# A short GpSimd memset behind each of 64 indirect transfers

## The chip, the cores and the metric

The kernel runs on one core of a Trainium2 chip. The metric is the device time of one execution in microseconds. Lower is better. The core has five engines with their own instruction queues: PE (TensorE, matmuls and transposes), DVE (VectorE), ACT (ScalarE), POOL (GpSimd) and SP (SyncE, which here only issues DMAs). Each queue runs in its written order, and semaphores order the queues against each other.

## The reference

A sequence model of four layers works on `x` of 4 x 1024 tokens x 128 features in float32. Each layer adds a mixing part and then a feed-forward part, with a layernorm behind each. Layer 1's feed-forward part and its neighbours are what matters here:

```python
x = _layernorm(x + _L1_attn_ref(...))     # a linear recurrence over the tokens
x = _layernorm(x + _L1_ffn_ref(...))      # 16 experts, 4 per token, and a shared expert
x = _layernorm(x + _L2_attn_ref(...))     # causal attention, 16 heads of 8
x = _layernorm(x + _L2_ffn_ref(...))      # 8 experts, 2 per token
```

```python
# _L1_ffn_ref, in short
topk_idx, tw = _route(x, router_w, bias)  # 4 of 16 experts from 2 of 4 groups, weights
h = einsum('td,edf->etf', x, gate_w); u = einsum('td,edf->etf', x, up_w)
y = einsum('etf,efd->etd', silu(h) * u, down_w)
routed = einsum('etd,te->td', y, combine) # combine: tw at the chosen experts
return routed + shared_expert(x)
```

The other layers are a gated scan and a quantized linear layer (layer 0), and a short Toeplitz mix with 32 experts (layer 3).

## The kernel before, in words

The tokens lie in SBUF as 32 tiles of 128 tokens. The experts are not computed for all tokens. For each layer with experts and each part of the tokens, the kernel writes a list of rows to DRAM, sorted by expert, and the experts read it back in groups of four tiles. Layer 1 has two parts: `a`, the first half of every sequence, and `r`, the second half. Their lists are called `l1ra` and `l1rr` (layer 1, rows, part). Layers 2 and 3 have three lists each.

- `l1_route` computes the router on DVE, and `positions` (line 1261) turns it into row numbers `posl1r` (line 1302).
- `spread` (line 1373) writes the list: for each of 16 tiles and each of 4 choices, one indirect DMA from `x` to the rows named by `posl1r`. That is 64 transfers of 128 rows. They are issued by `indirect` (line 1325, the DMA itself at line 1327) from the Pool queue[...].
- `gathered` (line 1388) reads a group of the list back as `xg`, by a DMA of the SP queue at line 1392. It waits for every transfer of the list, and for its buffer.
- `small_experts` (line 1781) transposes `xg` on PE (line 169) and runs the experts.

The order of work is written out by hand as generators. `mix` runs a main generator and lets a side generator step in by estimated times; whatever the side adds is ordered behind the latest instruction of the main one on the same engine. The estimate per transfer is `step`. Around the change, the main generator is layer 2's attention on the first half of the sequences, and the side is layer 1's routing and spreading of part `r`:

```python
self.run(self.mix(self.l2_attn(0), self.chain(self.l1_route(r), self.spaced(self.spread("l1", r, K1), 1, 2, 1.45))))
```

`spaced(..., 1, 2, 1.45)` sets `self.spacing`: every transfer waits for the landing of the one two before it (`before`, line 1345), and the planner counts 1.45 us for each. Part `a` is spread without it. `self.moved` holds the names of the latest transfers; each new one is ordered behind the last two of them in Pool's queue, without a semaphore. After this line come the experts of layer 1 on part `r`, with layer 2's routing and its list `l2ra` at their side.

Of the kernel before, what the change touches and what calls it, by code (L numbers as in the profile page):

```python
# [20 lines left out]
P = 128  # L21
# [35 lines left out]
class Part:  # L57
# [3 lines left out]
    def __init__(self, name, q0, nq, rows=None, lg0=None):  # L61
        self.name, self.q0, self.nq, self.lg0 = name, q0, nq, lg0
        if rows is None:
            self.order = list(range(q0 * QT, (q0 + nq) * QT))
        else:
            self.order = [tile_of(b, 2 * q + k) for b in rows for q in range(q0, q0 + nq) for k in range(2)]
        self.t0, self.nt = q0 * QT, len(self.order)
# [7 lines left out]
class Kernel:  # L75
    def __init__(self, ctx, tc, ins, out, cols, consts, rows):
        self.tc, self.nc, self.ins, self.out = tc, tc.nc, ins, out
        self.count = itertools.count()
        nc = self.nc
        self.const = self.pool(ctx, "const")  # L80
        self.small = self.pool(ctx, "small", 3)
        self.routes = self.pool(ctx, "routes")
        self.side = self.pool(ctx, "side", 2, space=PSUM)
        dram = self.pool(ctx, "dram", space=DRAM)

        self.cols_t = self.load(self.const, ins["cols"])
        self.cst_t = self.load(self.const, ins["consts"])
        self.x = self.tile(self.const, [P, NT, D], "x")
        self.xT = self.tile(self.const, [P, NT * P], "xT")
        nrow = ins["rows"].shape[1]  # L90
        self.rows_t = self.tile(self.const, [P, nrow], "rows")
        nc.gpsimd.dma_start(out=self.rows_t, in_=ins["rows"].to_broadcast([P, nrow]))
        self.col = {k: self.cols_t[:, a:b] for k, (a, b) in cols.items()}
        self.cst = {k: self.cst_t[:, a:b] for k, (a, b) in consts.items()}
        self.row = {k: self.rows_t[:, a:b] for k, (a, b) in rows.items()}
        self.ident = self.cst["ident"]
        self.eps = self.tile(self.const, [P, 1], "eps")
        nc.vector.memset(self.eps, LN_EPS)
        self.halfpi = self.tile(self.const, [P, 1], "halfpi")
        nc.vector.memset(self.halfpi, math.pi / 2)  # L100
        self.ones = self.tile(self.const, [P, E3], "ones")
        nc.vector.memset(self.ones, 1.0)
        self.rnd = self.tile(self.const, [P, 1], "rnd")
        nc.vector.memset(self.rnd, RND)
        self.drop = self.tile(self.const, [P, 1], "drop")
        nc.vector.memset(self.drop, -RND)
        self.zero = self.tile(self.const, [P, D], "zero")
        nc.gpsimd.memset(self.zero, 0.0)
        self.flag = self.tile(self.const, [1, 1], "flag", I32)
        self.hm = self.tile(self.const, [P, 4], "hmg")  # L110

        self.first, self.rest = Part("a", 0, 2), (Part("b", 2, 1), Part("c", 3, 1))
        self.parts = (self.first, *self.rest)
        self.by_rows = (
            Part("a", 0, 2, range(B), 0), Part("m", 2, 2, (0, 1), NT // 2), Part("n", 2, 2, (2, 3), 3 * NT // 4)
        )

        self.rows_done = 0

        self.listed = set()  # L120

        self.traced, self.latest = nc.cur_bb.bb.instructions, {}
        self.now = self.moved_by = 0.0
        self.moved = []
        self.landing = []
        self.spacing = None

        self.lists, self.route = {}, {}
        self.both = (self.first, Part("r", 2, 2))
        for lay, ne, k in (("l1", E1, K1), ("l2", E2, K2), ("l3", E3, K3)):  # L130
            for pt in {"l1": self.both, "l2": self.by_rows, "l3": self.parts}[lay]:
                tl = -(-((pt.nt * P * k + (P - 1) * ne) // P) // 4) * 4
                self.lists[lay, pt.name] = (
                    self.tile(dram, [tl * P, D], f"{lay}r{pt.name}"), self.tile(dram, [tl * P, D], f"{lay}y{pt.name}"), tl
                )
        self.wall2 = self.tile(dram, [P, E2 * 3 * F2], "wall2")
        self.xsave = self.tile(dram, [P, NT, D], "xsave")

        self.ksave = self.tile(dram, [P, B, BLK], "ksave")
        self.vsave = self.tile(dram, [P, B, 4, (NH + 1) * VW], "vsave")  # L140
# [1232 lines left out]
    def spread(self, lay, part, k):  # L1373

        pos, _, _, done, _ = self.route[lay + part.name]
        rows = self.lists[lay, part.name][0]
        for t in range(part.nt):
            for i in range(k):
                ins = self.indirect(
                    apart=done,  # L1380
                    out=rows, out_offset=bass.IndirectOffsetOnAxis(ap=pos[:, t, i : i + 1], axis=0),
                    in_=self.x[:, part.order[t], :], in_offset=None,
                )
                done.append(ins)
            yield (self.step * k,)
        self.listed.add(lay + part.name)

# [835 lines left out]
```

## Time and profile before

| what | value |
| --- | --- |
| median of 3 runs | 1930.79 us (1930.78 to 1932.56) |
| the profiled execution | 1937.33 us, of which the span is 1935.5 us |
| mean granted PE clock | 0.896 of full speed |
| Pool busy | 690.3 us, 36% of the span |
| transfers to `l1rr` | 64, 1022 ns of Pool each on the mean, from 629.0 to 723.7 us |

The span goes from the first to the last instruction of the profiled execution; about 1.8 us of its time lie around it. A row of the profile names the line, the engine, the operation and the tiles (output, arrow, inputs), then how many there were, how long they were busy in all, and the mean of one in ns. Idle time stands behind it with what ended it: a landing of a DMA, an instruction of another engine, or "issue" where the profile shows no wait. For a DMA, the row of the issuing engine only covers the issue; the landing comes later.

### The profile page before, as it was taken

What the parts mean: (1) busy time and instruction counts of PE and PEld (TensorE: products, weight loads), DVE (VectorE), ACT (ScalarE), POOL (GpSimd) and SP (SyncE); (2) the same over time, 40 slices, a digit from 0 to 9 for tenths busy, and PEclk for the clock granted to TensorE, in tenths of its full rate; (3) what the DMA queues carried; (4) which work ended last, traced back from release to release, by engine and by line L of the source; (5) the groups of instructions that cost most, each with busy time, mean ns of one, the idle gap of its engine ahead of it and who ended that gap; (6) DMA issues with size and microseconds to landing.
All of it is one profiled execution on the core that took longest, in us unless ns stands there. A gap on an engine that the chain in (4) does not pass through costs nothing. (4 is left out here: it accounts for less than half of the span.)

```text
span 1935.5 us, 27095 instructions
## 1 busy us (share of the span) xinstructions
PE 1541.5 (80%) x9025; PEld 920.8 (48%) x9025; DVE 1199.2 (62%) x3491; ACT 900.6 (47%) x1349; POOL 690.3 (36%) x670
## 2 busy tenths in 40 slices
PE   7885677597847887989977878798798998999850
PEld 3332433385423345856632232333355757768650
DVE  8998698465766664635564565546442446866383
ACT  5876265243324554423336756564532236644330
POOL 2000148604630660265443000030536430567775
PEclk9897688798978998999988988898988999989985
DMA  9990002244430113632241000000452213425452
GB/s 297 288 288 10 1 17 86 87 126 133 159 129 18 60 63 129 183 96 73 78 137 32 1 1 1 2 23 1 159 213 83 66 28 93 141 68 167 122 147 61
DMA packets 215530, 187.10 MB, mean 97 GB/s; under 512 B 16528, under 2 KB 194064, under 8 KB 214864
## 3 DMA queue, kind: packets, MB, share of 16 engines
q1 hardware_dynamic: 194672, 142.29, 23.6%
q0 software_dynamic: 20704, 42.86, 7.3%
q8 instruction: 84, 1.38, 0.3%
q14 instruction: 70, 0.57, 0.1%
HBM read 88.49 MB, written 96.60 MB: 96 GB/s over the span
## 5 line engine op out<-in xcount | busy, mean ns | idle before, releaser
L1081 ACT ACTIVATE pr<-sc 128x1024 f32<-128x1024 f32 x288 | 279.4, 1021 | 175.2 <-PE sc L161 174.8
L161 PE MATMUL sc<-qm,kT 32*128 32x512 f32 (+3 forms) x1536 | 197.7, 559 | 16.7 <-ACT pr L1081 16.7
L161 PE MATMUL s<-pr,va 128*32 128x512 f32 (+3 forms) x1536 | 167.5, 532 | 19.0 <-DVE x L1019 10.2
L161 PE MATMUL gu<-ld,xgT 128*128 x640 | 165.1, 400 | 10.2 <-DVE hg L1812 5.9
L1087 DVE TENSOR_TENSOR pr<-pr,ld 128x512 f32<-128x512 f32 (+1 forms) x160 | 91.7, 581 | 105.6 <-ACT pr L1081 105.4
L161 PE MATMUL gu<-wall,xgT 128*128 x304 | 148.2, 612 | 2.0 <-ACT xgT L171 2.0
L161 PEld LDWEIGHTS sc<-qm,kT 32*128 32x128 f32 x1536 | 83.7, 194 | 112.4 <-issue 61.1
L161 PEld LDWEIGHTS gu<-ld,xgT 128*128 128x128 f32 x640 | 119.5, 198 | 34.7 <-DVE hg L1812 6.1
L1812 DVE TENSOR_TENSOR hg<-sg,gu 128x256 f32<-128x256 f32 x160 | 66.0, 417 | 92.0 <-ACT sg L1811 91.6
L173 DVE COPY hT<-tp 128x512 f32<-128x512 f32 x118 | 80.9, 686 | 66.2 <-PE tp L169 66.2
L1567 ACT ACTIVATE sg<-gu 128x512 f32<-128x512 f32 x76 | 45.4, 597 | 144.7 <-PE gu L161 143.6
L1811 ACT ACTIVATE sg<-gu 128x256 f32<-128x256 f32 x160 | 61.3, 385 | 107.7 <-PE gu L161 79.8
L171 ACT COPY xgT<-tp 128x512 f32<-128x512 f32 x99 | 58.0, 586 | 99.9 <-PE tp L169 99.8
L1327 POOL DMA_INDIRECT l1ra<-x,posl1a x64 | 79.8, 1246 | 61.3 <-DVE peq L1321 42.0
L1327 POOL DMA_INDIRECT l1rr<-x,posl1r x64 | 65.4, 1022 | 100.9 <-DVE posl1r L1302 70.8
L169 PEld LDWEIGHTS tp<-ld,hg 128*128 128x128 f32 x624 | 77.4, 141 | 49.0 <-issue 32.5
L1569 DVE TENSOR_TENSOR hg<-sg,gu 128x512 f32<-128x512 f32 x76 | 51.8, 682 | 78.9 <-ACT sg L1567 78.8
L1327 POOL DMA_INDIRECT l2rm<-x,posl2m x16 | 15.7, 983 | 236.8 <-DVE peq L1320 230.1
L169 PE MATMUL tp<-ld,hg 128*128 128x128 f32 x624 | 96.4, 275 | 3.7 <-DVE hg L1812 2.0
L1327 POOL DMA_INDIRECT l3ra<-x,posl3a x64 | 63.7, 996 | 93.3 <-DVE usedl3a L1315 51.0
L161 PEld LDWEIGHTS s<-pr,va 128*32 128x32 f32 x1536 | 37.1, 113 | 122.6 <-issue 78.4
L161 PE MATMUL yp<-ld,hT 128*128 x640 | 86.1, 276 | 2.3 <-DVE mv L197 1.5
(447 smaller groups left out, 3439.1 us busy)
## 6 DMA issues: line engine op xcount, KB each, us to landing
wall<-wall SPq DMA_DIRECT2D x16, 768.0 KB, 7.8
l3ra<-zero SPq DMA_DIRECT2D x1, 6144.0 KB, 25.5
ld<-in_l_w SPq DMA_DIRECT2D x2, 3072.0 KB, 10.6
wall<-we SPq DMA_DIRECT2D x24, 256.0 KB, 2.1
ld<-in_l_w SPq DMA_DIRECT2D x1, 6144.0 KB, 20.6
l1ra<-zero SPq DMA_DIRECT2D x1, 5120.0 KB, 19.6
l1rr<-zero SPq DMA_DIRECT2D x1, 5120.0 KB, 23.1
xg<-l3ra SPq DMA_DIRECT2D x20, 256.0 KB, 2.9
```

Of the source, the lines that this page charges most:

```text
L161: return self.nc.tensor.matmul(out, lhsT, rhs, start=start, stop=stop)
L169: nc.tensor.transpose(pt[:, k * P : (k + 1) * P], s, self.ident)
L171: nc.scalar.copy(dst, pt[:, : n * P])
L173: nc.vector.tensor_copy(dst, pt[:, : n * P])
L1081: nc.scalar.activation(pr, sc[h], AF.Exp)
L1087: nc.vector.tensor_tensor(d, d, cst["tril"].unsqueeze(1).unsqueeze(1).to_broadcast([P, 2, n, P]), ALU.mult)
L1327: ins = self.nc.gpsimd.indirect_dma_start(**kw)
L1567: nc.scalar.activation(sg, gu[:, 0, :], AF.Silu)
L1569: nc.vector.tensor_tensor(h, sg, gu[:, 1, :], ALU.mult)
L1811: nc.scalar.activation(sg, pg[:, :, 0, :], AF.Silu)
L1812: nc.vector.tensor_tensor(h[:, 2 * c : 2 * c + 2, :], sg, pg[:, :, 1, :], ALU.mult)
```

## The change

A tile `idle` of 384 bytes per partition is added. Behind each transfer of the list `l1r` (layer 1, part `r`), and only where the spacing is set, Pool clears this tile with a memset. The memset is ordered behind its transfer, and, by its entry in `self.moved`, ahead of the next transfer, both without a semaphore. Nothing reads the tile.

```diff
@@ __init__
         self.eps = self.tile(self.const, [P, 1], "eps")
+        self.idle = self.tile(self.const, [P, 384], "idle", mybir.dt.uint8)
         nc.vector.memset(self.eps, LN_EPS)
@@ spread
                 done.append(ins)
+                if lay + part.name in ("l1r",) and self.spacing:
+                    stay = self.nc.gpsimd.memset(self.idle, 0)
+                    self.tc.add_manual_dep(
+                        stay.ins, ins.ins.name,
+                        mybir.DependencyInfo(mybir.DependencyClass.NoSync, mybir.DependencyReason.DATA),
+                        reason="queued behind",
+                    )
+                    self.moved.append(stay.ins.name)
             yield (self.step * k,)
```

## The prediction

> **What bounds the kernel now.** I read the page first, then the Pool timeline around the list that is touched, then the waits of the DMA queue that reads the list, then PE's timeline at the point where the list is first used.
>
> ```profile
> span 1935.5 us, 27095 instructions
> PE 1541.5 (80%) x9025; PEld 920.8 (48%) x9025; DVE 1199.2 (62%) x3491; ACT 900.6 (47%) x1349; POOL 690.3 (36%) x670
> ...
> L1327 POOL DMA_INDIRECT l1rr<-x,posl1r x64 | 65.4, 1022 | 100.9 <-DVE posl1r L1302 70.8 <-DMA l1rr<-x,posl1r 23.8 <-issue 6.4
> ```
>
> PE is the busiest engine; Pool is busy for a third of the span. The 64 transfers of layer 1's second list, l1rr, cost Pool 65.4 us of work, and 23.8 us of waiting are put down to landings. Pool's own timeline in that stage (start, duration, idle before):
>
> ```profile
> 635.58 0.95 POOL L1327 DMA_INDIRECT l1rr<-x,posl1r  x1 [0.30 <-DMA l1rr<-x,posl1r]
> 637.28 0.95 POOL L1327 DMA_INDIRECT l1rr<-x,posl1r  x1 [0.75 <-DMA l1rr<-x,posl1r]
> 640.50 0.95 POOL L1327 DMA_INDIRECT l1rr<-x,posl1r  x1 [2.26 <-DMA l1rr<-x,posl1r]
> 641.75 1.02 POOL L1327 DMA_INDIRECT l1rr<-x,posl1r  x1 [0.30 <-issue]
> ...
> 723.65 0.96 POOL L1327 DMA_INDIRECT l1rr<-x,posl1r  x1 [0.30 <-DMA l1rr<-x,posl1r]
> 805.14 0.95 POOL L1327 DMA_INDIRECT l2ra<-x,posl2a  x1 [80.52 <-DVE posl2a L1302]
> ```
>
> The usual step is 1.26 us: 0.96 of work and a gap of 0.30 that is there whoever is named as its releaser. Only what lies above 0.30 is a true wait for a landing: eleven gaps, 11.0 us above their 0.30 in all (0.45, 1.96, 0.52, 0.73, 2.07, 0.44, 1.56, 0.31, 1.52, 0.87, 0.59). So the list runs from 629.0 to 723.65 (first and last start), 94.6 us. After it Pool has nothing to do until 805.14, and what it does then waits for DVE: no later work of Pool is queued close behind the list.
>
> Who waits for the list? The SP queue, which loads it back for the experts (xg, line 1392), and behind that PE's transposes of xg (waits as total us, times, longest):
>
> ```profile
> SPq L1392 <- DMA l1rr<-x,posl1r: 20.5, 4, 13.4
> SPq L1392 <- PE s L169: 19.5, 1, 19.5
> ...
> 745.48 2.79 SPq L1392 DMA_DIRECT2D xg<-l1rr  x3
> ...
> 754.60 1.88 PE L161 MATMUL s<-ld,t 128*128 128x8 f32 x8 [0.68 <-ACT t L171]
> 756.34 1.95 PE L169 MATMUL tp<-ld,xg 128*128 128x128 f32 x8
> ...
> 724.70:745.50 20.80, 18.22 (x196) 9.94 (x192) 12.15 (x45) 12.23 (x16) 0.00 (x0) 1.00 0.01 4
> 745.50:756.10 10.60, 3.80 (x19) 3.19 (x20) 5.50 (x28) 1.15 (x2) 0.00 (x0) 0.75 0.68 225
> ```
>
> SP first waits for the landings and then 19.5 us more for a PE transpose that frees the buffer. The list's last landing took 2.9 us from its issue (the view of l1rr from 715 to 760), so it was down at 726.6; the loads went out at 745.48 because of the buffer. The first three xg loads landed 2.9 us after issue (view of xg, 740 to 750), the first at 748.4, but PE used it at 756.1 (its weight load), without a wait, since its queue still held the tail of the attention. The stage's end is set by PE and DVE in the attention (PE busy 18.22 of 20.80 us, then the norm on DVE), not by the list. The last landing may therefore move from 726.6 to 745.5 + (756.1 - 748.4) = 753.1 before PE loses anything: **26.5 us of cover**.
>
> **The change, part by part.** It adds 64 Pool memsets of 128x384 bytes, one after each l1rr transfer, in Pool's program order. The instruction orders of PE, DVE, ACT and SP are the same apart from names, with the same waits; on Pool the memsets alternate with the transfers, and one l1rr transfer loses a wait on Pool's own counter (another wait pair, on PE and ACT, goes from a later l2ym gather; the trace shows no wait there for either). A tile of 384 bytes per partition is added. The planned step of 1.45 us per transfer is unchanged, so nothing else is moved. Queued behind each memset is only the next transfer; behind the last one, l2ra, 57 us later than anything here.
>
> What is one memset worth? The nearest rows:
>
> ```profile
> L344 POOL MEMSET keep<- 128x1024 f32 x1 | 1.0, 955 | 0.0
> L108 POOL MEMSET zero<- 128x128 f32 x1 | 0.2, 232 | 0.0
> L2213 POOL MEMSET const-uint8-127<- 128x1 uint8 x1 | 0.1, 103 | 0.0
> ...
> 7.43 0.95 POOL L344 MEMSET keep<- 128x1024 f32 x1
> 8.44 0.10 POOL L345 MEMSET keep<- 128x4 f32 x1
> ```
>
> Slope (955 - 232) / 896 = 0.807 ns per f32 element; 384 elements are 232 + 256 x 0.807 = 439 ns. That takes a byte as dear as a word. If the bytes went as 96 words it would be about 0.20 us: the low end. The high end is 0.50 + 0.30 = 0.80, where the transfer's 0.30 gap is paid once more on the way into and out of the memset. No row shows a memset between two indirect transfers.
>
> First rule weighed. The row's duration gives 0.44 per memset. The Trainium skill, "Perfetto Trace Analysis", section "GPSIMD Engine Instruction", says that a GpSimd row's span is not to be trusted and that one should take start-to-start distances. In this trace that is 8.44 - 7.43 = 1.01 against a duration of 0.955, so 0.06 more: 0.50. The sum by each: the list has 63 steps; a transfer waits for the landing of the one two before it, so two memsets lie in every such wait and take away up to twice their length from each of the eleven waits. With 0.44: 63 x 0.44 = 27.7, less 7.4 taken away, 20.3 us longer, 6.2 of the cover left. With 0.50: 31.5 less 7.9, 23.6 us longer, 2.9 left. I take 0.50, the dearer: last transfer at 747.3, landed at 750.2, first xg at 753.1, PE needs it at 756.1. **Cost on the path: nothing**; the cover is the buffer's release at 745.48 and PE's queue up to 756.1. At 0.20 the list grows by 8.3 us, at 0.80 by 50.4 - 10.2 = 40.2, which is 13.7 past the cover. The cover is used up at 0.55 per memset (34.6 - 8.3 = 26.3), and 0.2% (3.9 us, about what a measurement of this kernel can tell from no change) is reached at 0.62. That is a thin margin: 0.05 us per memset is 3 us.
>
> Second rule weighed, one that speaks against the change. DVE's rows in the stage: L964 tensor_scalar takes 482 ns at the median and 622 at most, L213 346 and 546, with Pool busy for 65 of 95 us; over the 16 of them (means 498 and 390 ns) that is 8 x 0.016 + 8 x 0.044 = 0.5 us above the medians. The Trainium skill, "SBUF — State Buffer", section "Who interferes with whom", says that DVE in a two-port mode and GpSimd lock each other out for a whole instruction. By the rule all 20 such DVE instructions between 629 and 748 could wait a whole memset, 20 x 0.5 = 10 us, some of it before PE transposes; by the row, 32 us more of Pool work adds 0.5 x 32 / 65 = 0.25 us. I take the row. The other way round, Pool's transfers were lengthened by 4 us over their 0.96; the memsets may be too by a share (2 us), which would eat most of the 2.9 left.
>
> Sum: the profiled execution took 1937.33 us (span 1935.5 and 1.8 around it); the runs' median is 1930.79. Only the difference is carried over: 0 for the memsets, about 1 us for brushes with DVE and the thin margin: 1932.
>
> **The rivals.**
>
> *The memset costs more than 0.62 us each, and the list becomes the bound.* One mechanism: each hand-over between transfer and memset pays the 0.30 gap again. The place is SP's wait for the last landing at line 1392 and then PE's first transpose of xg at 756.1. With 0.80 the last landing is at 766.8 and PE starts 13.7 us late; the stage behind it has PE busy 68.5 of 73.9 us and would not make it good: 1930.8 + 13.7 = 1944.5. For it: every transfer here shows that 0.30 even with nothing to wait for. Against: around the direct transfers at the kernel's start the next memset begins with no gap. It decides from 0.55, and counts from 0.62.
>
> *Faster, by the granted clock.* In 745.5 to 756.1 the clock is 0.75, in the 59 us before the list 0.82, over the whole run 0.896. Shifted work can meet the half-speed phases elsewhere; the same program took 6.5 us more in the profiled execution than in the median run, so moves of this size occur. 5 us less: 1926. Against: nothing in the change saves work, and waits of Pool that vanish here were not on the path.
>
> *The change does not do what it says.* The memsets could be so short (0.20) that only the landing waits are filled: 1930.8. It gives the forecast's side.
>
> **How the numbers follow.** Hidden or nearly so (memset below 0.62): 0.46. List past its cover by more than 3.9 us: 0.39, since the margin is thin and three small costs point one way; most of it between 1935 and 1945. Faster by clock: 0.15. The likeliest is 1932, its own range 1927 to 1934.6. The range that holds 8 in 10 takes in the rival at 0.80 nearly whole, and most of the clock's: 1927 to 1944.
>
> **What would show it.** Right: memset rows of about 0.44 us, l1rr steps near 1.76 us, last transfer near 747, landing waits above 0.30 down to about 3 us, xg loads a few us after 745.5, PE's first tp<-ld,xg without a wait on DMA xg at about 756. Wrong: steps above 1.9 us, PE waiting for DMA xg at that transpose, or DVE's tensor_scalar rows clearly above 0.48 us in the stage. A difference with none of these would have to be in the clock row.

## The result, and the profile after

| kernel | median | runs |
| --- | --- | --- |
| before | 1933.76 us (1927.75 to 1941.34) | 14 |
| with the memsets | 1939.64 us (1935.14 to 1947.70) | 14 |

The ratio is 1.0039, 95% interval 1.0024 to 1.0053: slower by about 7 us on the means, and the whole interval lies above 1. The profiled execution took 1947.7 us, the longest of the 14, so its own excess (10 us over the profiled one of before) is larger than the typical one.

One fact has to be known before the experiments are read. Chips differ: the same kernel before takes about 1930 us on the chips of this table and on chip 4, and about 2250 us on chips 3, 10 and 14. Every ratio below is against the kernel before on the same chip. I call the two sorts chips of sort A and of sort B. Ratios leave out slow runs, those over 1.5% above the fastest of their kernel on that chip, so they can differ from the quotient of the medians; the executions profiled for e2_tiny, e3_words and e6_nl_after were such runs.

The page's first lines, after:

```profile
span 1945.9 us, 27157 instructions
PE 1545.9 (79%) x9025; PEld 924.1 (47%) x9025; DVE 1202.3 (62%) x3491; ACT 900.8 (46%) x1349; POOL 718.0 (37%) x734
```

Pool is 27.7 us busier: the 64 memsets, 28.4 us, less a little on the transfers. The view of the tile `idle` and Pool's timeline (start, duration, idle before):

```profile
L1387 POOL MEMSET idle<- x64: 432/432/587, 629.8 to 736.5; 128x384 uint8 x64
...
640.82 0.96 POOL L1328 DMA_INDIRECT l1rr<-x,posl1r  x1 [0.17 <-issue]
641.78 0.43 POOL L1387 MEMSET idle<- 128x384 uint8 x1
642.38 0.96 POOL L1328 DMA_INDIRECT l1rr<-x,posl1r  x1 [0.17 <-issue]
...
735.58 0.96 POOL L1328 DMA_INDIRECT l1rr<-x,posl1r  x1 [0.17 <-issue]
```

A memset takes 0.43 us and starts the moment the transfer's row ends; the gap ahead of the next transfer shrinks from 0.30 to 0.17. So the step goes from 1.26 to 1.57 us, 0.31 more. The list runs from 628.6 to 735.58.

Did anyone wait for it? The SP queue's waits, its loads of `xg`, and PE's first use of them:

```profile
SPq L1401 <- DMA l1rr<-x,posl1r: 26.3, 4, 18.0
SPq L1401 <- PE s L170: 17.5, 1, 17.5
...
755.40 2.79 SPq L1401 DMA_DIRECT2D xg<-l1rr  x3
...
766.27 1.95 PE L170 MATMUL tp<-ld,xg 128*128 128x128 f32 x8
```

No. After the last landing SP still waits 17.5 us for the buffer, and PE's transpose has no wait in front of it. But the buffer's release has itself slid from 745.48 to 755.40 (9.9 us), and so has PE's first use, from 756.34 to 766.27. When PE's matmuls are matched one by one between the two traces, the later one is 2.0 us early at 650, 6.2 late at 701, 9.9 late at 753 and 10.6 late at the end: nearly all of the difference arises beside the list, in layer 2's attention. Two things have changed there. First, rows of DVE, which has no new work (name, count, ns min/median/max, time of first and last; kernel before, then after):

```profile
L964 DVE TENSOR_SCALAR qm<-qT,hmg x8: 466/482/622, 660.0 to 699.7; 128x512 f32<-128x512 f32 x8
L213 DVE TENSOR_SCALAR x<-x,mv,rstd x12: 340/344/546, 651.1 to 729.4; 128x128 f32<-128x128 f32 x12
```

```profile
L965 DVE TENSOR_SCALAR qm<-qT,hmg x8: 468/738/1029, 657.9 to 705.6; 128x512 f32<-128x512 f32 x8
L214 DVE TENSOR_SCALAR x<-x,mv,rstd x12: 339/483/810, 649.9 to 736.0; 128x128 f32<-128x128 f32 x12
```

The shortest are as short as before; the others are longer by up to more than a memset. The means go from 498 to 744 ns (eight of them, +2.0 us) and from 374 to 529 ns (twelve, +1.9 us). Second, the granted clock. The same 693 matmuls of the stage, before and then after (window, length, busy time and count of PE, PEld, DVE, ACT and Pool, then PE's clock, DMA share and GB/s):

```profile
665.00:704.00 39.00, 33.81 (x319) 17.01 (x318) 25.46 (x70) 22.40 (x26) 25.17 (x26) 1.00 0.18 66
704.00:745.50 41.50, 35.31 (x374) 18.88 (x372) 22.89 (x69) 25.31 (x31) 14.51 (x14) 1.00 0.11 43
```

```profile
665.00:710.00 45.00, 38.64 (x317) 18.71 (x317) 26.89 (x68) 22.51 (x26) 37.88 (x54) 0.87 0.15 58
710.00:755.40 45.40, 38.39 (x376) 20.06 (x374) 23.83 (x69) 25.30 (x30) 22.98 (x32) 0.92 0.11 44
```

PE is busy 77.0 us where it was 69.1 (+7.9), at a clock of 0.87 and 0.92 where it was 1.00; its idle time grows by 2.0. The clock accounts for the longer busy time by itself: 33.81 / 0.87 = 38.9 and 35.31 / 0.92 = 38.4. In this execution, then, most of the excess is a half-speed phase that fell into the stage. Over all 14 runs the part of the clock is smaller: their mean clock is 0.8951, against 0.8977 in 23 runs of before on chip 4, and by a straight line through those 23 a thousandth of clock goes with 1.0 us. That is an estimate of 2.6 us out of 7, and a weak one: the two means need not come from the same chip.

### The profile page after: what moved, and what is told of

The parts are those of the page before. It is cut to its first block, busy times and chain, and to the rows that moved or that the text cites. A ratio compares the mean times of both kernels' runs of the same rounds, so it can differ in the third digit from the quotient of the medians.

```text
span 1945.9 us, 27157 instructions
## 1 busy us (share of the span) xinstructions
PE 1545.9 (79%) x9025; PEld 924.1 (47%) x9025; DVE 1202.3 (62%) x3491; ACT 900.8 (46%) x1349; POOL 718.0 (37%) x734
## 6 DMA issues: line engine op xcount, KB each, us to landing
ld<-in_l_w SPq DMA_DIRECT2D x2, 3072.0 KB, 10.6
```

## The experiments

The theories at the start: **port** (memset and DVE's tensor_scalar exclude each other), **clock** (the shifted work meets more half-speed phases), and **list** (the longer list is waited for, which the waits above already speak against). After the first four runs came a fourth, **fetch**: while the transfers follow each other closely, loads of instructions come late on some chips and the engines stand idle. Its part without the cause, that a wider step of the transfers ends such idle stretches, I call **spacing**.

**The change again, one-byte and word memsets, and two memsets (chip 3, sort B).** The first of the four, the changed kernel unedited:

> The changed kernel once more, beside the next three. Port theory (each memset holds a port that DVE's two-operand-port tensor_scalar needs, and those instructions stand in front of PE in the attention): the rows L965 qm and L214 x are again well above the 482 and 344 ns of before, near 740 and 480 at the median, and the time is 0.3 to 0.5% above before. Clock theory (the difference is only where the half-speed phases of PE fell in one execution): the DVE rows still grow, but the attention stage 629 to 755 us changes by less than 3 us when the granted clock of the stage is the 0.95 of before, and the ratio comes back towards 1.000 to 1.002. List theory (the longer list is waited for): PE waits for DMA xg at its first transpose of the list; the first profile did not show that.

Measured: 2199.26 us against 2276.22, ratio 0.9686 (0.9621 to 0.9752). Faster by 3%. No theory had this. The memsets take 432 ns here too, and the masks beside them 676 ns on the mean, so DVE is held up on this chip as well, and something larger is gained.

```diff
@@ e2_tiny
-                    stay = self.nc.gpsimd.memset(self.idle, 0)
+                    stay = self.nc.gpsimd.memset(self.idle[:, 0:1], 0)
@@ e3_words
-        self.idle = self.tile(self.const, [P, 384], "idle", mybir.dt.uint8)
+        self.idle = self.tile(self.const, [P, 96], "idle")
```

> The same 64 memsets and the same tile, but each clears one byte per partition (about 0.1 us instead of 0.43). Port theory: qm under 520 ns and x under 380 at the mean, ratio 1.000 within 0.15%. A theory that the tile's place, the extra instructions or the waits that the order lost are what costs: ratio as of the change, 1.003 to 1.005. List theory: list 629 to about 724, ratio 1.000.

Measured: 2272.17 us, ratio 0.9995 (0.9933 to 1.0057). The memset takes 116 ns, the list runs 672.0 to 761.6 (1.42 us a step), the mask rows stay at 482 ns. Neither cost nor gain.

> The same 384 bytes as 96 float32 words: about 0.21 us each by the row of 128 words (232 ns). Port theory: half the holding time, qm near 580 to 620 ns at the mean, ratio 1.001 to 1.003. Clock theory: anything within 0.2% of 1, unrelated to the memset's length. List theory: list ends near 729, ratio 1.000.

Measured: 2264.71 us, ratio 0.9858 (0.9755 to 0.9962), with runs from 2224 to 2293; the medians are 0.5% apart. The memset takes 193 ns, so the price goes by elements, not bytes; the list runs 671.7 to 761.5 and the mask rows stay at 481 ns. Its profiled execution loses as much in the list's stage as the kernel before does on chip 14 (below), so whether there is a small gain stays open.

```diff
@@ e4_two
-                    stay = self.nc.gpsimd.memset(self.idle, 0)
+                    for _ in range(2):
+                        stay = self.nc.gpsimd.memset(self.idle, 0)
...
```

> Two memsets of 384 bytes behind each transfer: the step grows to about 2.0 us. Port theory: Pool holds the port for about 55 us, qm near 900 ns or more at the mean, ratio 1.006 to 1.010. List theory: the list's last landing moves to about 759, past what PE can absorb (753 in the profile of before, about 763 if the attention itself is 10 us later): a wait of PE for DMA xg of 0 to 7 us, ratio 1.000 to 1.004 if that alone costs. Clock theory: no more than the change itself, 1.002 to 1.005.

Measured: 2215.16 us, ratio 0.9764 (0.9701 to 0.9827), list 668.0 to 801.4. The doubled list still costs little: PE waits 1.1 us for `xg`. So the clear gain comes at a step somewhere between 1.43 and 1.70 us, and a step of 2.1 us is no better.

**What a chip of sort B loses (chip 14).** The kernel before itself:

> The kernel before, unchanged, for a profile on the chip of these runs. Fetch theory (formed on the last four runs: while the list's transfers follow each other at 1.27 to 1.42 us, the loads of instructions for DVE, ACT and PE come late on some chips, and the engines stand idle with nothing that they wait for): where the time of before is near 2270 us, DVE and PE show gaps of 30 to 50 us between 660 and 770 us that end with no releaser; where it is near 1930 us, no gap over 10 us there. Port and clock theories: no such gaps on any chip.

Measured: 2246.99 us. Matched by PE's matmuls against the trace of before on sort A, this execution loses 63.2 us between 650 and 701 of that trace's time, which is the list's stage. The same difference is 66.5 in e2_tiny and 66.7 in e3_words, but 5.7 in e1_again, 2.9 in e4_two and 1.8 in e8_again. The timelines of ACT and DVE there:

```profile
704.28 1.02 ACT L1081 ACTIVATE pr<-sc 128x1024 f32<-128x1024 f32 x1 [19.41 <-remote]
756.83 1.02 ACT L1081 ACTIVATE pr<-sc 128x1024 f32<-128x1024 f32 x1 [37.94 <-remote]
...
757.89 0.69 DVE L1087 TENSOR_TENSOR pr<-pr,ld 128x512 f32<-128x512 f32 x1 [47.22 <-ACT pr L1081]
```

ACT stands still for 38 us and the trace has no releaser for it ("remote"); DVE waits for ACT. The kernel with one-byte memsets shows the same on three engines at once:

```profile
758.76 2.08 PE L162 MATMUL s<-xT,w 128*128 128x512 f32 x2 [38.67 <-issue]
758.51 0.19 DVE L909 COPY lg<-s 128x32 f32<-128x32 f32 x1 [48.26 <-remote]
746.51 0.59 ACT L1111 COPY oc<-s 128x512 f32<-128x512 f32 x1 [29.44 <-remote]
764.92 1.94 ACT L1082 ACTIVATE pr<-sc 128x1024 f32<-128x1024 f32 x2 [17.82 <-remote]
```

They stop at different times (720, 710 and 717). PE and DVE resume within half a microsecond, ACT does one copy at 746.5 and resumes at 764.9: all near the end of the list, whose last transfer starts at 761.6. One candidate is the loading of instructions, which goes through DMA queues too. The DMA view of the same window, 708 to 772, of the kernel before (e5_before) and then of the changed kernel (e8_again, below) (queue, packets, MB, share of the 16 engines):

```profile
DMA packets 1059, 2.17 MB, mean 34 GB/s; under 512 B 530, under 2 KB 530, under 8 KB 1059
q0 software_dynamic: 1059, 2.17, 8.6%
```

```profile
DMA packets 1535, 3.43 MB, mean 54 GB/s; under 512 B 656, under 2 KB 656, under 8 KB 1529
q0 software_dynamic: 1216, 2.49, 9.9%
q1 hardware_dynamic: 313, 0.86, 3.5%
q8 instruction: 4, 0.07, 0.4%
q14 instruction: 2, 0.02, 0.1%
```

With the kernel before, 64 us pass without one instruction load and the data queue q1 stands as well; with the memsets between, six loads come through. In records of single loads, q8 loads come every 14 to 21 us where the work runs, while e5_before has none from 706.6 to 775.1. Against reading this as proof: an engine that stands still may ask for no instructions; in e2_tiny one load, of q14, does come in the middle, at 739.1; and the engines of e5_before resume at 756.8 and those of e2_tiny at 758.5, while the next recorded loads are at 773.2 and 776.4. That the engines stand still, and that the wider step ends it, is shown; that they wait for instructions is my reading of it.

**The changed kernel on the same chip, and port taken out.**

> The changed kernel again, beside the others of this call. Fetch theory: ratio 0.965 to 0.975 where before is near 2270, 1.002 to 1.005 where it is near 1930. Clock theory: ratio anywhere within 1% of 1, not the same sign twice on one kind of chip. Port theory: 1.003 to 1.005 on every chip.

Measured: 2174.04 us against 2244.80, ratio 0.9712 (0.9665 to 0.9758), list 669.0 to 776.1, and no idle stretch on PE, DVE or ACT while it runs is longer than 6.5 us; those without a releaser stay under 0.9 us.

```diff
@@ e6_nl_after and e11_nl_after2: the norm step on DVE, and the head masks
+                nc.vector.scalar_tensor_tensor(x, x, mv[:, t, 0:1], rstd[:, t : t + 1].to_broadcast([P, D]), ALU.subtract, ALU.mult)
...
-                        nc.vector.tensor_scalar(qm[:, m, :], qT, self.hm[:, m : m + 1], None, ALU.mult)
+                        nc.vector.tensor_tensor(qm[:, m, :], qT, self.hm[:, m : m + 1].to_broadcast([P, BLK]), ALU.mult)
```

> The changed kernel with DVE's masks (line 965) and the norm's last step (line 214, where the norm runs on DVE alone) written as two-input operations[...]: 0.69 instead of 0.48 us for a mask by the row of L1088 with the same shape. Port theory: these rows are then no longer than that beside the memsets (mask mean under 0.72, norm step under 0.35 us), and on a chip with before near 1930 the ratio is lower than that of the change or equal to it (1.000 to 1.004), the slower forms costing back some 2 us. Clock theory: the rows say nothing of the time. Fetch theory: on a chip with before near 2270 the ratio stays near 0.97.

Measured: 2184.87 us, ratio 0.9693 (0.9640 to 0.9746). The groups of DVE in the stage (count, then busy us, mean ns, idle before), this kernel and then e8_again:

```profile
L967 DVE TENSOR_TENSOR qm<-qT,hmg 128x512 f32<-128x512 f32 x8 | 5.0, 686 | 0.1
L214 DVE SCALAR_TENSOR_TENSOR x<-x,mv,rstd 128x128 f32<-128x128 f32 x16 | 4.7, 354 | 0.1
```

```profile
L965 DVE TENSOR_SCALAR qm<-qT,hmg 128x512 f32<-128x512 f32 x8 | 4.4, 607 | 0.1
L214 DVE TENSOR_SCALAR x<-x,mv,rstd 128x128 f32<-128x128 f32 x16 | 5.3, 483 | 0.1
```

As instructions that read two tensors these rows no longer stretch: the norm step stays at 354 ns instead of 483, the masks at 680 to 694 ns, and the longest memset falls from 580 to 443 ns. That a memset and a tensor_scalar hold each other up is thereby shown, in both directions. The two kernels' ratios overlap, so what it costs in time cannot be read from this chip, where one execution differs from the next by 2%.

**A memset behind every indirect transfer, all layers.**

```diff
@@ e7_all and e12_all2, in indirect (the memsets in spread are dropped)
-        self.moved = self.moved[-130:] + [ins.ins.name]
+        stay = self.nc.gpsimd.memset(self.idle, 0)
+        self.tc.add_manual_dep(stay.ins, ins.ins.name, behind, reason="queued behind")
+        self.moved = self.moved[-130:] + [ins.ins.name, stay.ins.name]
```

> The memset behind every indirect transfer of the kernel, lists and gathers (some 590 run). Fetch theory: on a chip with before near 2270 the idle gaps of the last third (1650 to 2200 us) shrink, and the time falls to 1950 to 2120, well below the changed kernel. On a chip with before near 1930: slower by 1 to 4%, since Pool's queue of gathers is on the way of the experts' ends, with 0.48 us more for each transfer. Port and clock theories: slower on every chip.

Measured: 2017.18 us, ratio 0.8994 (0.8959 to 0.9028), at a mean clock of 0.883 in the profiled execution where e5_before had 0.846. The last layer's transfers (1650 to 1865 us of sort A's time) cost e5_before, e2_tiny and e8_again 133 to 138 us more there than before's trace on the chip of sort A, this one about 4. The same work in before on sort A, in e5_before and in this kernel (columns as above):

```profile
1650.00:1865.00 215.00, 196.74 (x1126) 157.86 (x1125) 130.58 (x387) 103.08 (x199) 149.77 (x151) 0.95 0.45 129
```

```profile
1826.00:2175.00 349.00, 225.87 (x1127) 175.44 (x1127) 130.81 (x387) 101.62 (x199) 146.30 (x152) 0.80 0.28 80
```

```profile
1680.00:1898.70 218.70, 199.37 (x1126) 158.76 (x1125) 133.08 (x387) 102.92 (x199) 183.93 (x260) 0.95 0.42 121
```

Of the 134 us in e5_before, 105 are idle time of PE (18, 123 and 19 us in the three) and 29 longer busy time, at a clock of 0.80 against 0.95. The loss goes where the step is widened, and nothing else was changed there: this is the strongest evidence for spacing. What was not tried is a pause of the same length without a memset.

**Back on sort A (chip 4).** What of the +0.39% is the memset's presence, and what its length?

```diff
@@ e9_four: four memsets behind every fourth transfer; e10_tiny: as e2_tiny
-                if lay + part.name in ("l1r",) and self.spacing:
-                    stay = self.nc.gpsimd.memset(self.idle, 0)
+                if lay + part.name in ("l1r",) and self.spacing and i == k - 1:
+                    for _ in range(4):
+                        stay = self.nc.gpsimd.memset(self.idle, 0)
...
```

> The one-byte memsets again, for a second chip. On a chip with before near 1930: port theory 1.000 within 0.15%, with mask rows at 0.48 us; if the tile's place, the added instructions or the lost waits cost, 1.003 to 1.005. On a chip with before near 2250: fetch theory 0.995 to 1.005, the stall of 40 to 60 us in the list still there.

Measured: 1932.83 us, ratio 1.0002 (0.9989 to 1.0015), mean clock 0.8975. Landing waits fall as in the changed kernel (9.0 us in 8 waits), and the rows are undisturbed:

```profile
L965 DVE TENSOR_SCALAR qm<-qT,hmg x8: 481/482/487, 658.4 to 698.0; 128x512 f32<-128x512 f32 x8
L214 DVE TENSOR_SCALAR x<-x,mv,rstd x12: 340/343/501, 650.4 to 727.6; 128x128 f32<-128x128 f32 x12
```

So the added tile, 64 more instructions, their order and the lost waits cost nothing that shows (within 0.15%): it is the memset's length.

> The same 64 memsets in lumps: four behind every fourth transfer of the list (the last of each tile), none behind the others. The list is as long as with the change (about 105 us), but three of four transfers follow each other at 1.27 us. Fetch theory, on a chip with before near 2250: if the mean rate counts, the stall is gone and the ratio 0.965 to 0.98; if each transfer needs its own gap, a part of the stall stays and the ratio is 0.98 to 1.0. On a chip with before near 1930: 1.002 to 1.006, as the change, by the port theory (the same holding time); no gap over 10 us in the list's stage.

Measured: 1936.83 us, ratio 1.0020 (1.0002 to 1.0037), mean clock 0.8968. The same memset time in 16 blocks stretches few rows (masks 510 ns on the mean, norm step 354) and costs about half. This list is the longest of the three, 631.0 to 746.6, so the cost does not go by the length of the list alone. The order of the three is the same in time, in stretched rows and in clock (0.8975, 0.8968, 0.8951). The intervals of e9_four and of the changed kernel overlap. Whether on sort B the mean rate counts or each gap, which this kernel was also to tell, stays open.

**Both edits once more (chip 10, sort B).**

> The same edit as e6_nl_after: the head masks by tensor_tensor and the vector-engine norm step by scalar_tensor_tensor, with the 64 memsets kept. Port theory: the mask rows stay at about 684 ns and the norm row at about 350 ns, as they did there; since the mask by tensor_tensor is itself about 200 ns dearer than an undisturbed mask (684 against 482 ns, x8 = 1.6 us in the list's stage) while the lengthening it avoids was 2.0 us on the masks and 1.9 us on the norm steps, the time against before should be between -0.1% and +0.3%, so about 2 to 6 us under the changed kernel's +7 us at most. Clock rival: the +0.39% came from the clock granted in the stage; then the time stays at +0.3 to +0.5% whatever the vector engine's rows show. Fetch theory: on a chip where the kernel before takes about 2250 us, -3% again (2185 us), since the gaps between transfers are the same; on one where it takes 1930 us it says nothing.

> The same edit as e7_all: a memset behind every indirect transfer of all layers. Fetch theory: on a chip where the kernel before takes about 2250 us, about -10% again (2020 us), because every stretch of transfers that follow without a gap loses its stall; on one where it takes 1930 us there are no such stalls to lose, and the cost is what the memsets add: lists of 64 with +0.31 us a step, 20 us each, hidden or not as each list's cover is, and longer vector-engine rows beside them: +1 to +4% (1950 to 2010 us). Clock rival: spacing alone raises the mean granted clock; then the time would fall on both sorts of chip. Port rival: the time rises on both sorts, which e7_all already contradicts on one.

Measured, against 2269.63 us: 2209.44 us, ratio 0.9745 (0.9693 to 0.9796), and 2014.77 us, ratio 0.8899 (0.8858 to 0.8941). Both repeat chip 14, in the rows of e11_nl_after2 too (masks 686 ns, norm step 357, longest memset 444). The question that was meant for sort A, whether the time goes back to that of before once the rows no longer stretch, is not answered.

## Why the prediction was right and wrong

- **Range, right; likeliest case, wrong.** 1939.6 lies in 1927 to 1944, but the likeliest case, hidden at no cost, did not come. Slower had a chance of 0.39, by a mechanism that did not act. That the time still fell into the range is partly luck: the upper end was drawn for a list that PE waits for.
- **Length of a memset, right; its price in the step, wrong.** 0.44 was forecast from the slope of two f32 rows, 0.444 is the mean. I added 0.06 for the distance from start to start and used 0.50. The runs show 0.31, because the gap in front of the next transfer falls by 0.13. The Trainium skill's advice in "Perfetto Trace Analysis", section "GPSIMD Engine Instruction", to use start-to-start distances, was sound as a way to measure; the failing was to measure it between two memsets and not to ask whether the transfer's own gap would stay. The list grew by 12.3 us, not 23.6.
- **The cover, right, with more to spare.** The last landing was expected at 750.2; it came at 737.9, 17.5 us ahead of the buffer. The rival of a gap paid twice was wrong in sign: the gap became smaller. e4_two doubled the memsets without a large wait.
- **The DVE term, wrong: the step that failed.** I weighed the rule of the Trainium skill, "SBUF — State Buffer", section "Who interferes with whom", against the rows of before, and took the rows: 0.25 us. Those rows stood beside indirect transfers, which hardly stretch DVE's instructions (a mask takes 482 ns at the median and 622 at most), and I scaled them by Pool's busy time as if a memset did the same. The rule speaks of GpSimd's instructions in general, the memset with them. The runs show 3.9 us on 20 rows, a good third of the rule's upper 10, and the stretching disappears with one-byte memsets and with instructions that read two tensors. What should have warned me is that no row of before showed a memset beside a tensor_scalar.
- **The clock rival, wrong in sign.** It was put at 5 us faster. The mean clock fell by about 0.0026 instead, by the slope 2.6 us. With 3.9 us of stretched rows this comes near the 7 us found, but the split is attributed, not shown: in the profiled execution PE's idle time in the stage grew by only 2.0 us, how much of the 3.9 lies on the path was not isolated on sort A, and why the clock fell is open.
- **Sure of the sign on one sort of chip only.** Nothing in the trace of before hinted at chips where the list stops other engines. There the change is about 3% faster: 0.9686 and 0.9712 as it stands, 0.9693 and 0.9745 with the mask and norm rows rewritten, on three chips. A forecast from sort A's trace alone had no ground for it.

## What to carry to other kernels

When an instruction is placed on GpSimd because that engine has time, ask which instructions of VectorE run beside it, and take the cost from a row of the same pairing, not from GpSimd work of another kind. A wait that nobody on the path feels is no free place: here the list stayed hidden and the kernel lost 0.39% beside it. Before tuning the spacing of indirect transfers, look on more than one chip at the engines beside them for long idle stretches that no instruction released.

## What was not expected of the hardware

On two chips of sort B, 3 and 14, indirect transfers of the list that follow each other at 1.32 to 1.43 us leave PE, DVE and ACT idle for up to 39, 48 and 38 us at a time; at 1.70 us and above (a memset of 0.43 us between) they do not, on chip 10 neither, where the closer step was timed but not profiled. A memset behind each of them in all layers takes the kernel from 2245 to 2017 us and from 2270 to 2015 us there. On sort A the list's stage shows no such stretch at 1.26 us (6.8 us at most), and what the version with a memset behind every transfer takes there was not measured. What differs between the chips is open.

Memset time on GpSimd went by elements: 116 ns for 1 byte per partition, 193 ns for 96 f32, 432 ns for 384 bytes. The gap of 0.30 us ahead of an indirect transfer falls to 0.17 to 0.19 us at the median behind any of these memsets.
